# Six layer norms and a head norm: inverse roots moved from GpSimd's power to ScalarE's logarithm and exponential, with a new order of the units

## The chip, the cores and the metric

The kernel runs on one core of one Trainium2 chip. The core has five engines that matter here, each with its own queue of instructions that it serves in order: TensorE (PE in the profile, with its weight loads as PEld), VectorE (DVE), ScalarE (ACT), GpSimd (POOL) and SyncE (SP), which issues the transfers. They wait for each other by semaphores. The metric is the device time of one execution in microseconds (us), the median of several runs.

## The reference

32 graphs of 512 nodes with 256 features go through four layers, each followed by a residual and a layer norm without gain:

```python
def _layernorm(x, axis=-1, eps=1e-5):
    m = jnp.mean(x, axis=axis, keepdims=True)
    v = jnp.var(x, axis=axis, keepdims=True)
    return (x - m) / jnp.sqrt(v + eps)

x = _layernorm(x + _L0_gnn_ref(x, adj, ...))   # 4 heads, attention over edges; norm per head, eps 1e-6
x = _layernorm(x + _L1_gnn_ref(x, adj, W, a))  # 1 head, ELU
x = _layernorm(x + _L2_gnn_ref(x, adj, ...))   # 8 heads, symmetric mask, feed forward of 1024, two norms inside
x = _layernorm(x + _L3_gnn_ref(x, adj, W, a))  # 1 head, leaky
```

So a graph has six norms over 256 features (after layer 0; after layer 1; two inside layer 2; after layer 2; after layer 3) and one norm over the 64 features of each of 4 heads in layer 0. The two in the feed forward that follow each other (the second norm inside layer 2, then that after the residual) have only a gain and an addition between them.

## The kernel before, in words

The kernel first runs `fast_path`, which is right for adjacencies of zeros and ones and for sums that stay in range. It gathers a verdict on the way (`sums`, `ok`), and only where that fails `general_path` runs. In the runs shown only the fast path is executed.

The 512 rows of a graph stand as four blocks of 128 partitions (`R` = 4), features in the free dimension. Every stage of a graph is a Python generator that yields between *units*, small pieces of TensorE work with what belongs to them:

- **edges, x**: load the transposed adjacency in two halves (`adjt`, turned to bytes on ACT with a sum of its entries and of their squares), the features and their transpose.
- **layer 0**: `h0p` (four projections), then for each of four heads `gp` (a row of exponentials spread over the partitions), `pt` (line 393, the unnormalised attention on DVE, four per head), `o` (four times 128x65). Then the head norm (`head_layernorm`) and the norm of the layer (`layernorm`).
- **layer 1** and **layer 3**: `xt1p`/`xt3p` (two units that transpose the normed rows through PE), `h1p`/`h3p` (four projections, copied out of PSUM by ACT on line 333), `gp`, `pt`, `o` (four units, one per block of rows). In layer 1 ACT evaluates a relu and an exponential per block (lines 476, 477), in layer 3 DVE adds the residual (line 674). Then a norm each.
- **mask**: the symmetric mask `a2`, on DVE.
- **qkv**: `xt2p`, `qkp` (four units), `vp`. **attention**: for each of four pairs of heads four units `s` (the scores, exponentials on ACT in line 553, product with the mask on DVE in line 556; the last of the four has the mask `shut` added on PE) and one unit `cp`. **projection**: `ctp` (transposes, also for `ct`, which the prediction calls ctp2 where the two are told apart), `wop`.
- **feed forward**: a norm, `ytp` (transposes), then eight times `f1p` (first product, relu on ACT in line 638 to `ft`) and `f2p` (second product). Then a norm, line 654 (gain), line 655 (residual), and another norm.

A `layernorm` on four blocks: DVE takes statistics of each block (lines 266, 267), adds eps (line 269), GpSimd takes the power -0.5 of a 128x4 tile (line 270), DVE multiplies by the negated mean (line 271), and ACT writes the four blocks one after the other (line 275). `head_layernorm` has sums on DVE, squares on ACT (line 294), a sum of those on DVE (line 295), then scale and eps (line 296), the power of a 128x16 tile on GpSimd (line 297) and a product on DVE (line 298).

**What sets the order.** Some 3.5 graphs are in work at once. Each unit has a place in the table `PLACES`, a number of the planner's time; a unit of graph b stands at `PERIOD * b` plus its place, and the units of all 32 graphs are merged by these numbers:

```python
with tc.manual_schedule(engines={mybir.EngineType.PE}):
    for _ in heapq.merge(*(graph(b) for b in range(B))):
        pass
```

TensorE's instructions stand in exactly that order. Those of the other engines are placed by the tile framework's scheduler, except for a few that are pinned behind the last product (`in_place`). Transfers are all issued by SP.

PSUM has eight banks, given out by stage: two to layers 0 and 1 (with edges and x), four to the middle (qkv, attention, projection), two to feed forward and layer 3 (`bank` takes `n = 4 if stage[0] == "b" else 2`). A product that needs a bank waits until what was in it has been copied out. So within layer 3 the third `h3p` needs the bank of the first, and `gp` that of the third.

Of the kernel before, what the change touches and what calls it, by code (L numbers as in the profile page):

```python
# [27 lines left out]
PLACES = {  # L28
    "edges": [-1440, -1440, -410, 1420],
    "x": [3260],  # L30
    "mask": [16220, 16520, 16600, 17520],
    "layer 0": [
        2410, 3594, 4534, 4534, 5073, 5753, 5753, 5823, 6123, 6123, 6233, 6233, 6603, 6773, 6903,
        7687, 7687, 7777, 8077, 8077, 8157, 8287, 8439, 8439,
    ],
    "layer 1": [11037, 11066, 11277, 11729, 11849, 11879, 12043, 13286, 13554, 14195, 14884],
    "qkv": [17180, 17740, 18270, 18270, 18270, 18990, 19484, 19654, 21635, 21635],
    "attention": [
        20262, 20932, 21922, 21982, 22092, 22092, 22092, 22350, 22350, 23077, 23537, 23537,
        24028, 24208, 24328, 24532, 25064, 25220, 25368, 25943,  # L40
    ],
    "projection": [26801, 26801, 26861, 26911, 27661, 27721, 28721, 29140, 29256, 29848],
    "feed forward": [
        31013, 31120, 32042, 32263, 32263, 32465, 32710, 33771, 33983, 34076, 34284, 34691,
        35070, 35329, 35615, 36103, 36646, 37299,
    ],
    "layer 3": [39714, 39714, 40906, 41226, 41406, 41526, 41526, 42359, 42359, 42379, 42379],
}
# [4 lines left out]
RD_MIN = 1e-25  # L53
RD_MAX = 1e25


# [16 lines left out]
def fast_path(ctx: ExitStack, tc: tile.TileContext, a: dict, out: bass.AP, bad: bass.AP):  # L73
# [21 lines left out]
    VC = DH + 1  # L95
    ND = R * (H + 2 + H2)

    const = ctx.enter_context(tc.tile_pool(name="const", bufs=1))
    latest = [None]
# [25 lines left out]
    nc.vector.tensor_copy(identb, ident)  # L125
    mhalf = const.tile([P, R * H], F32, name="mhalf")
    nc.gpsimd.memset(mhalf, -0.5)
    ok = const.tile([P, ND], F32, name="ok")
    nc.gpsimd.memset(ok, 1.0)
# [129 lines left out]

    def layernorm(y, eps):  # L260

        st = buf([P, R, 6], "bn", "bn", 2)
        mv = buf([P, R, 2], "mv", "mv", 2)
        rs = buf([P, 3, R], "rs", "rs", 2)
        for r in range(R):
            nc.vector.bn_stats(st[:, r, :], y[:, r, :])  # L266
            nc.vector.bn_aggr(mv[:, r, :], st[:, r, :])
        var = mv[:, :, 1]
        nc.vector.scalar_tensor_tensor(rs[:, 0, :], var, eps, var, op0=ALU.add, op1=ALU.max)  # L269
        nc.gpsimd.tensor_tensor(rs[:, 1, :], rs[:, 0, :], mhalf[:, :R], op=ALU.pow)  # L270
        nc.vector.scalar_tensor_tensor(  # L271
            rs[:, 2, :], mv[:, :, 0], -1.0, rs[:, 1, :], op0=ALU.mult, op1=ALU.mult
        )
        for r in range(R):
            nc.scalar.activation(  # L275
                y[:, r, :],
                y[:, r, :],
                AF.Identity,
                bias=rs[:, 2, r : r + 1],
                scale=rs[:, 1, r : r + 1],  # L280
            )

    def head_layernorm(y, eps):

        G = R * H
        yg = y.rearrange("p r (g d) -> p (r g) d", g=H)
        st = buf([P, 3, G], "lnh", "st", 2)
        nc.vector.tensor_reduce(st[:, 0, :], yg, axis=X, op=ALU.add)
        nc.vector.tensor_scalar_mul(st[:, 0, :], st[:, 0, :], 1.0 / HO)
        nc.vector.tensor_sub(yg, yg, st[:, 0, :].unsqueeze(2).to_broadcast([P, G, HO]))  # L290
        for i in range(2):
            g = slice(i * G // 2, (i + 1) * G // 2)
            sq = part("sq").rearrange("p (g d) -> p g d", d=HO)
            nc.scalar.activation(sq, yg[:, g, :], AF.Square)
            nc.vector.tensor_reduce(st[:, 1, g], sq, axis=X, op=ALU.add)
        nc.vector.tensor_scalar(st[:, 1, :], st[:, 1, :], 1.0 / HO, eps, op0=ALU.mult, op1=ALU.add)
        nc.gpsimd.tensor_tensor(st[:, 2, :], st[:, 1, :], mhalf[:, :G], op=ALU.pow)  # L297
        nc.vector.tensor_mul(yg, yg, st[:, 2, :].unsqueeze(2).to_broadcast([P, G, HO]))

# [96 lines left out]

    def layer0(x, xt, at, rd):
        h = yield from project(xt, w0, D + 2 * H, "h0")
# [39 lines left out]
        nc.vector.tensor_add(y, y, h[:, :, :D])  # L438
        head_layernorm(y, 1e-6)
        nc.vector.tensor_mul(y, y, all_rows(gam0))  # L440
        nc.vector.tensor_add(y, y, x)
        layernorm(y, 1e-5)
        return y
# [15 lines left out]

    def layer1(x, at, rd):  # L460
        xt = yield from transposed([x[:, r, :] for r in range(R)], "xt1")
        h = yield from project(xt, w1g, D + 2, "h1")
        ex = buf([P, 2, R, 1], "ex", "ex1", 2)
        nc.scalar.activation(ex[:, 0], h[:, :, D : D + 1], AF.Exp, scale=-1.0)
        nc.scalar.activation(ex[:, 1], h[:, :, D + 1 :], AF.Exp)
        nc.gpsimd.memset(h[:, :, D : D + 1], 1.0)
        gb = yield from along(ex[:, 0], "gb1")
        pt = [kept("pt1", gb, at[:, j, :], ex[:, 1, j, :]) for j in range(R)]

        for r in range(0, R, 2):  # L470
            y, m = (part(n).rearrange("p (r d) -> p r d", d=D) for n in ("relu", "exp"))
            for i in range(2):
                p = yield from attend(pt, h, r + i, "o1")
                rdr = rd[:, r + i : r + i + 1]
                nc.vector.reciprocal(rdr, p[:, D : D + 1])
                nc.scalar.activation(y[:, i, :], p[:, :D], AF.Relu, scale=rdr)
                nc.scalar.activation(m[:, i, :], p[:, :D], AF.Exp, scale=rdr)
            nc.vector.scalar_tensor_tensor(y, m, 1.0, y, op0=ALU.min, op1=ALU.add)
            xr = x[:, r : r + 2, :]
            nc.vector.scalar_tensor_tensor(xr, y, -1.0, xr, op0=ALU.add, op1=ALU.add)  # L480
        layernorm(x, 1e-5)
        return x
# [131 lines left out]

    def feed_forward(x, y):
        layernorm(y, 1e-5)
        yt = yield from transposed([y[:, r, :] for r in range(R)], "yt")
# [4 lines left out]
        for r in range(0, R, 2):  # L622
# [29 lines left out]
            nc.vector.tensor_add(yr, acc, yr)  # L652
        layernorm(y, 1e-5)
        nc.vector.tensor_mul(y, y, all_rows(ln2g))
        nc.vector.tensor_add(y, y, x)
        layernorm(y, 1e-5)
        return y


    def layer3(x, at, rd):  # L660
        xt = yield from transposed([x[:, r, :] for r in range(R)], "xt3")
# [9 lines left out]
        for r in range(R):  # L671
# [4 lines left out]
            )  # L676
        layernorm(x, 1e-5)
        return x
# [11 lines left out]

    def layer0_all(b, x, xt, at, rd):
        if b == 0:
            bcast(bet0, "bet0")
            bcast(gam0, "gam0")
        return (yield from layer0(x, xt, at, rd))

    def layer1_all(b, x, at, rd):
        if b == 0:
            weights13(w1g, "w1g", "a1")
        return (yield from layer1(x, at, rd))  # L700

# [10 lines left out]

    def feed_forward_all(b, x, y):
        if b == 0:
            weights_ff()
        return (yield from feed_forward(x, y))

    def layer3_all(b, x, at, rd):
        if b == 0:
            weights13(w3g, "w3gt", "a3")  # L720
        return (yield from layer3(x, at, rd))

    def graph(b):
        yield PERIOD * b + PLACES["edges"][0]
        rd = sb.tile([P, ND], F32, tag="rd", name="rd", bufs=3)
        rds = [rd[:, ends[i] : ends[i + 1]] for i in range(4)]
        if b == 0:
            xt, x = yield from paced(b, "x", load_x(b))
        at = yield from paced(b, "edges", mask(b))
        if b:  # L730
            xt, x = yield from paced(b, "x", load_x(b))
        x = yield from paced(b, "layer 0", layer0_all(b, x, xt, at, rds[0]))
        x = yield from paced(b, "layer 1", layer1_all(b, x, at, rds[1]))
        a2 = yield from paced(b, "mask", symmetric(b, at))
        qk = yield from paced(b, "qkv", qkv_all(b, x))
        cs = yield from paced(b, "attention", attention(qk, *a2))
        y = yield from paced(b, "projection", attended_all(b, x, cs, rds[2]))
        x = yield from paced(b, "feed forward", feed_forward_all(b, x, y))
        x = yield from paced(b, "layer 3", layer3_all(b, x, at, rds[3]))
        nc.sync.dma_start(out[b].rearrange("(r p) d -> p r d", p=P), x)  # L740
        nc.vector.scalar_tensor_tensor(ok, rd, RD_MIN, ok, op0=ALU.is_ge, op1=ALU.mult)
        nc.vector.scalar_tensor_tensor(ok, rd, RD_MAX, ok, op0=ALU.is_le, op1=ALU.mult)

# [657 lines left out]
```

## Time and profile before

| what | value |
|---|---|
| median of 3 runs | 3909.93 us (3907.24, 3909.93, 3911.33) |
| span of the profiled execution | 3904.6 us (its own time is not listed apart; the three runs lie 2.6 to 6.7 us above the span) |
| PE busy | 3753.3 us, 96% |
| DVE busy | 2674.8 us, 69% |
| ACT busy | 1926.2 us, 49% |
| POOL busy | 346.9 us, 9% |
| mean granted clock of TensorE | 0.983 |
| transfers | 261.20 MB, 23.1% of the DMA engines' time in the one hardware queue |

In the profile each engine's busy time is the union of its instructions. A group is named by its line, engine, operation and `out<-in` by the program's tile names. Lines of PE are all line 102, the helper that issues products, so one goes by the tile names. Behind the bar of a group stand its busy time, the mean of one in ns, and the engine's idle time ahead of it with what ended it. In a timeline the columns are start and length in us, engine, line, operation and tiles; in square brackets the engine's idle time ahead and what released it. A float32 product shows as two passes.

### The profile page before, as it was taken

The page shows a single profiled execution, that of the slowest core. Times are in us where ns is not written, and L with a number is a line of the kernel's source. Part 1 is how long each engine was busy: PE and PEld are TensorE (multiplying, and loading weights), DVE is VectorE, ACT ScalarE, POOL GpSimd, SP SyncE. Part 2 cuts the span into 40 slices and gives each one's busy share as a digit, 9 for nine tenths or more (in the row PEclk, how much of TensorE's full clock was granted, in tenths as well). Part 3 has the DMA queues.
Part 4 walks back from the last instruction along what each step waited for, and adds up shares of the span by engine and source line. Part 5 has one row for each costly group of instructions (what it writes and reads, how often), then busy time and mean ns, then how long its engine had stood idle before and what let it go on. Part 6 is the DMA issues. An engine that isn't in the chain of part 4 may idle for free.

```text
span 3904.6 us, 53602 instructions
## 1 busy us (share of the span) xinstructions
PE 3753.3 (96%) x19238; PEld 2824.5 (72%) x19238; DVE 2674.8 (69%) x5594; ACT 1926.2 (49%) x4257; POOL 346.9 (9%) x266
## 2 busy tenths in 40 slices
PE   5899999999999999999999999999999999999996
PEld 4577777777777777777777777777777777777764
DVE  4667676677677677677677677677777677777653
ACT  2444455444455544455544455545555544555442
POOL 0000010000010001010001010001010001010000
PEclk6899999999999999999999999999999999999998
DMA  3222222222222222222222222222222222221120
GB/s 106 77 73 65 72 58 67 71 76 67 70 60 65 71 76 69 68 62 63 71 76 71 66 63 64 69 76 71 66 65 65 65 76 74 63 67 58 49 54 12
DMA packets 180431, 261.20 MB, mean 67 GB/s; under 512 B 36800, under 2 KB 72768, under 8 KB 180160
## 3 DMA queue, kind: packets, MB, share of 16 engines
q1 hardware_dynamic: 180160, 257.71, 23.1%
q8 instruction: 155, 2.54, 0.3%
q14 instruction: 116, 0.95, 0.1%
HBM read 106.57 MB, written 16.78 MB: 32 GB/s over the span
## 4 chain that ended last, share of the span: by engine, by line
PE 60%; DVE 14%; issue 8%; ACT 5%; POOL 5%; POOLq 0%; ACTq 0%
PE o L102 16%; PE f1p L102 7%; PE f2p L102 6%; PE qkp L102 5%; PE cp L102 5%; DVE pr L556 4%; ACT y L275 4%; POOL rs L270 3%; PE h3p L102 3%; PE s L102 3%; PE h1p L102 3%; PE wop L102 3%; POOL st L297 2%; PE gp L102 2%; PE vp L102 2%
## 5 line engine op out<-in xcount | busy, mean ns | idle before, releaser
L556 DVE TENSOR_TENSOR pr<-pr,a 128x1024 f32<-128x1024 f32 x384 | 459.1, 1216 | 319.3 <-ACT pr L553 319.2
L275 ACT ACTIVATE y<-y,rs 128x256 f32<-128x256 f32 x768 | 398.4, 589 | 438.2 <-DVE rs L271 438.2
L393 DVE SCALAR_TENSOR_TENSOR pt<-gb,ex,at 128x512 f32<-128x512 f32 x768 | 530.6, 744 | 77.6 <-ACT gb L345 77.6
L553 ACT ACTIVATE pr<-s 128x512 f32<-128x512 f32 x1024 | 545.2, 613 | 7.4 <-PE s L102 7.3
L102 PEld LDWEIGHTS o<-hv,pt 128*128 128x128 f32 x4096 | 508.4, 199 | 23.7 <-issue 8.4
L102 PE MATMUL o<-hv,pt 128*128 128x65 f32 x4096 | 502.7, 280 | 9.7 <-DVE pt L393 9.7
L102 PE MATMUL f2p<-wf,ft 128*128 128x256 f32 x2048 | 491.6, 383 | 12.3 <-ACT ft L638 12.2
L102 PE MATMUL cp<-pr,v 128*64 128x512 f32 x2048 | 474.9, 600 | 17.8 <-DVE pr L556 17.1
L102 PE MATMUL f1p<-yt,wf 128*128 128x256 f32 x2048 | 488.9, 381 | 0.3 <-DVE yt L302 0.3
L102 PE MATMUL o<-h,pt 128*128 128x257 f32 x2048 | 482.8, 383 | 3.7 <-DVE pt L393 3.7
L102 PEld LDWEIGHTS o<-h,pt 128*128 128x128 f32 x2048 | 381.5, 190 | 96.0 <-issue 40.6
L270 POOL TENSOR_TENSOR rs<-rs,mhalf 128x4 f32<-128x4 f32 x192 | 246.2, 1282 | 2118.8 <-DVE rs L269 1826.0
L638 ACT ACTIVATE ft<-f1p,cols 128x256 f32<-128x256 f32 x512 | 215.2, 474 | 442.2 <-PE f1p L102 442.2
L102 PEld LDWEIGHTS f2p<-wf,ft 128*128 128x128 f32 x2048 | 380.1, 191 | 69.5 <-ACT ft L638 17.1
L102 PEld LDWEIGHTS f1p<-yt,wf 128*128 128x128 f32 x2048 | 385.3, 191 | 54.5 <-DVE yt L302 0.8
L102 PE MATMUL s<-qk 128*128 128x512 f32 x1024 | 395.1, 481 | 1.6 <-ACT pr L553 1.6
L102 PEld LDWEIGHTS cp<-pr,v 128*64 128x64 f32 x2048 | 133.0, 136 | 286.0 <-issue 194.2
L266 DVE BATCH_NORM_STATS2 bn<-y 128x6 f32<-128x256 f32 x768 | 294.6, 411 | 4.5
L102 PEld LDWEIGHTS s<-qk 128*128 128x128 f32 x1024 | 187.8, 190 | 99.3 <-issue 40.6
L102 PE MATMUL qkp<-xt,wqkv 128*128 128x512 f32 x512 | 231.3, 594 | 0.0
L345 ACT COPY gb<-gp 128x512 f32<-128x512 f32 x192 | 111.5, 581 | 219.4 <-PE gp L102 219.4
L428 DVE RECIPROCAL rd<-o 128x4 f32<-128x4 f32 x128 | 23.4, 183 | 272.7 <-PE o L102 272.7
(134 smaller groups left out, 4582.5 us busy)
## 6 DMA issues: line engine op xcount, KB each, us to landing
qk<-hi SPq DMA_DIRECT2D x1024, 64.0 KB, 2.0
qk<-lo SPq DMA_DIRECT2D x1024, 64.0 KB, 2.0
adjt<-in_adjt SPq DMA_DIRECT2D x64, 512.0 KB, 3.5
adj<-in_adj SPq DMA_DIRECT2D x64, 512.0 KB, 3.6
xt<-in_xt SPq DMA_DIRECT2D x32, 512.0 KB, 3.4
x<-in_x SPq DMA_DIRECT2D x32, 512.0 KB, 4.7
out<-y SPq DMA_DIRECT2D x32, 512.0 KB, 3.0
wf<-in_w1t SPq DMA_DIRECT2D x1, 1024.0 KB, 7.6
```

The lines of the kernel that those rows point to most:

```text
L102: latest[0] = what(*args, **kwargs).ins.name
L266: nc.vector.bn_stats(st[:, r, :], y[:, r, :])
L270: nc.gpsimd.tensor_tensor(rs[:, 1, :], rs[:, 0, :], mhalf[:, :R], op=ALU.pow)
L275: nc.scalar.activation(y[:, r, :], y[:, r, :], AF.Identity, bias=rs[:, 2, r : r + 1], scale=rs[:, 1, r : r + 1],)
L297: nc.gpsimd.tensor_tensor(st[:, 2, :], st[:, 1, :], mhalf[:, :G], op=ALU.pow)
L345: nc.scalar.copy(g, p)
L393: nc.vector.scalar_tensor_tensor(t, g, f, edges, op0=ALU.max, op1=ALU.mult)
L428: nc.vector.reciprocal(rdh, o[:, :, HO:])
L553: nc.scalar.activation(t[:, i, :], s, AF.Exp, scale=QSCALE)
L556: nc.vector.tensor_mul(t, t, edges)
L638: nc.scalar.activation(ft[:, f, :], p[:, f, :], AF.Relu, bias=bf1[:, ff + f : ff + f + 1])
```

## The change

All inverse roots go to ScalarE, as exp(-0.5 ln(variance + eps)). The table set that holds both functions is loaded at the start. The add of eps moves into the logarithm's bias, the head norm's factor 1/64 into the scale of its square. Means and variances of all norms of a graph are kept in one tile `mvs` (three buffers), and at the end of a graph DVE checks that the variances are at most 1e18, beside the check of the denominators that was there. `PLACES` has new numbers for nearly all units, so TensorE's order changes. The scratch for GpSimd's own transfers is set to 8192.

The core of the diff (left out: arguments `mv`, `var` handed through the stages, and the rest of the table):

```diff
 PLACES = {
-    "edges": [-1440, -1440, -410, 1420],
-    "x": [3260],
+    "edges": [-2144, -1150, -1132, 1169],
+    "x": [2625],
...
-    "projection": [26801, 26801, 26861, 26911, 27661, 27721, 28721, 29140, 29256, 29848],
+    "projection": [26272, 26272, 26332, 26382, 27451, 27561, 28792, 29200, 29412, 29811],
     "feed forward": [
-        31013, 31120, 32042, 32263, 32263, 32465, 32710, 33771, 33983, 34076, 34284, 34691,
-        35070, 35329, 35615, 36103, 36646, 37299,
+        30548, 31062, 31829, 32245, 32245, 32541, 32692, 33753, 33965, 34306, 34732, 34800,
+        35052, 35117, 35751, 36541, 37158, 37317,
     ],
-    "layer 3": [39714, 39714, 40906, 41226, 41406, 41526, 41526, 42359, 42359, 42379, 42379],
+    "layer 3": [39718, 39718, 40714, 40734, 40817, 41334, 41569, 42319, 42319, 42339, 42339],
 }
...
+    NL = 6
+    NV = R * (NL + H)
+
+    nc.scalar.preload_act_table_set("natural_log_exp_and_others")
...
-    mhalf = const.tile([P, R * H], F32, name="mhalf")
-    nc.gpsimd.memset(mhalf, -0.5)
-    ok = const.tile([P, ND], F32, name="ok")
+    eps = {}
+    for e in (1e-5, 1e-6):
+        eps[e] = const.tile([P, 1], F32, name=f"eps{e}")
+        nc.gpsimd.memset(eps[e], e)
+    ok = const.tile([P, ND + NV], F32, name="ok")
...
-    def layernorm(y, eps):
+    def inverse_root(out, variance, e):
+        nc.scalar.activation(out, variance, AF.Ln, bias=eps[e])
+        nc.scalar.activation(out, out, AF.Exp, scale=-0.5)
+
+    def layernorm(y, e, mv):
 
         st = buf([P, R, 6], "bn", "bn", 2)
-        mv = buf([P, R, 2], "mv", "mv", 2)
-        rs = buf([P, 3, R], "rs", "rs", 2)
+        rs = buf([P, 2, R], "rs", "rs", 2)
         for r in range(R):
             nc.vector.bn_stats(st[:, r, :], y[:, r, :])
             nc.vector.bn_aggr(mv[:, r, :], st[:, r, :])
-        var = mv[:, :, 1]
-        nc.vector.scalar_tensor_tensor(rs[:, 0, :], var, eps, var, op0=ALU.add, op1=ALU.max)
-        nc.gpsimd.tensor_tensor(rs[:, 1, :], rs[:, 0, :], mhalf[:, :R], op=ALU.pow)
+        inverse_root(rs[:, 0, :], mv[:, :, 1], e)
         nc.vector.scalar_tensor_tensor(
-            rs[:, 2, :], mv[:, :, 0], -1.0, rs[:, 1, :], op0=ALU.mult, op1=ALU.mult
+            rs[:, 1, :], mv[:, :, 0], -1.0, rs[:, 0, :], op0=ALU.mult, op1=ALU.mult
         )
...
-            nc.scalar.activation(sq, yg[:, g, :], AF.Square)
-            nc.vector.tensor_reduce(st[:, 1, g], sq, axis=X, op=ALU.add)
-        nc.vector.tensor_scalar(st[:, 1, :], st[:, 1, :], 1.0 / HO, eps, op0=ALU.mult, op1=ALU.add)
-        nc.gpsimd.tensor_tensor(st[:, 2, :], st[:, 1, :], mhalf[:, :G], op=ALU.pow)
-        nc.vector.tensor_mul(yg, yg, st[:, 2, :].unsqueeze(2).to_broadcast([P, G, HO]))
+            nc.scalar.activation(sq, yg[:, g, :], AF.Square, scale=HO**-0.5)
+            nc.vector.tensor_reduce(var[:, g], sq, axis=X, op=ALU.add)
+        inverse_root(st[:, 1, :], var, e)
+        nc.vector.tensor_mul(yg, yg, st[:, 1, :].unsqueeze(2).to_broadcast([P, G, HO]))
...
         nc.sync.dma_start(out[b].rearrange("(r p) d -> p r d", p=P), x)
-        nc.vector.scalar_tensor_tensor(ok, rd, RD_MIN, ok, op0=ALU.is_ge, op1=ALU.mult)
-        nc.vector.scalar_tensor_tensor(ok, rd, RD_MAX, ok, op0=ALU.is_le, op1=ALU.mult)
+        okd, oks, okv = ok[:, :ND], ok[:, ND : ND + NL * R], ok[:, ND + NL * R :]
+        nc.vector.scalar_tensor_tensor(okd, rd, RD_MIN, okd, op0=ALU.is_ge, op1=ALU.mult)
+        nc.vector.scalar_tensor_tensor(okd, rd, RD_MAX, okd, op0=ALU.is_le, op1=ALU.mult)
+        variances = mvs[:, 1 : 2 * NL * R : 2]
+        nc.vector.scalar_tensor_tensor(oks, variances, VAR_MAX, oks, op0=ALU.is_le, op1=ALU.mult)
+        nc.vector.scalar_tensor_tensor(okv, var, VAR_MAX, okv, op0=ALU.is_le, op1=ALU.mult)
...
-    nc = bacc.Bacc("TRN2", target_bir_lowering=False, num_devices=1)
+    nc = bacc.Bacc("TRN2", target_bir_lowering=False, num_devices=1, dynamic_dma_scratch_size=8192)
```

Around the two norms of the feed forward, TensorE's units in the middle of the run stand as follows, from the built programs (the number is the graph's; `x` with a number means so many in a row):

```
before: 15:f2p 17:o1 16:s+shut 17:o1 16:cp 17:o1 16:ctpx4 17:o1 18:h0p 15:xt3px2 16:ctp2 18:h0p 16:ctp2 18:h0px2 16:wop 15:h3p 16:wop 15:h3p 18:gp0 16:wop 15:h3px2 15:gp3 17:xt2px2 16:wop 18:o0x4
after:  15:f2p 16:s+shut 17:o1 16:cp 17:o1 16:ctpx4 18:h0p 17:o1 18:h0p 16:ctp2x2 15:xt3px2 18:h0px2 15:h3px2 18:gp0 15:h3p 16:wopx2 15:h3p 16:wop 15:gp3 17:xt2p 18:o0x2 16:wop 18:o0 17:xt2p 18:o0
```

## The prediction

> **What bounds the kernel now.** I read the page's busy lines first, then the table by stretches, then PE's waits, then the timeline of one period.
>
> ```profile
> PE 3753.3 (96%) x19238; PEld 2824.5 (72%) x19238; DVE 2674.8 (69%) x5594; ACT 1926.2 (49%) x4257; POOL 346.9 (9%) x266
> ```
>
> ```profile
> 0.00:122.00 122.00, 77.25 (x302) 62.19 (x302) 56.55 (x107) 30.48 (x66) 8.70 (x14) 0.69 0.32 100
> 122.00:244.00 122.00, 112.69 (x572) 81.78 (x572) 78.46 (x143) 49.51 (x105) 8.10 (x5) 0.92 0.28 77
> 244.00:3660.00 3416.00, 3362.45 (x17510) 2539.54 (x17509) 2425.99 (x5078) 1753.29 (x3884) 315.12 (x233) 1.00 0.24 68
> 2044.80:2161.60 116.80, 115.10 (x603) 86.99 (x604) 83.12 (x175) 60.03 (x134) 10.76 (x8) 1.00 0.24 68
> 3782.00:3904.60 122.60, 83.15 (x336) 60.78 (x334) 47.68 (x128) 33.35 (x75) 7.87 (x7) 0.87 0.03 10
> ```
>
> (Stretch, length, then busy us of PE, PEld, DVE, ACT, POOL, granted clock, DMA share, GB/s.) PE is the bound: from 244 to 3660 us it idles 1.6%, at full clock, and the timeline repeats every 116.8 us, one graph. Only the first two and the last stretch are different: 54 us without PE work in them at the start, 39 at the end, and a granted clock of 0.69, 0.92 and 0.87. So the sum has three terms: what PE waits for in a period (about 29 times), the fill and the drain.
>
> The built order of the changed kernel has the same 11,539 matmuls on PE as before, so PE's work itself neither shrinks nor grows; only waits can move. Those of one period, in the timeline:
>
> ```profile
> 1948.93 0.16 DVE L269 SCALAR_TENSOR_TENSOR rs<-mv 128x4 f32<-128x4 f32 x1
> 1949.23 1.01 POOL L270 TENSOR_TENSOR rs<-rs,mhalf 128x4 f32<-128x4 f32 x1 [8.01 <-DVE rd L587]
> ...
> 1950.27 0.16 DVE L271 SCALAR_TENSOR_TENSOR rs<-mv,rs 128x4 f32<-128x4 f32 x1 [0.99 <-POOL rs L270]
> ...
> 1950.47 2.08 ACT L275 ACTIVATE y<-y,rs 128x256 f32<-128x256 f32 x4 [1.11 <-DVE rs L271]
> ...
> 1951.12 0.33 PE L102 MATMUL xt3p<-ident,y 128*128 128x128 f32 x1
> ...
> 1951.61 0.33 PE L102 MATMUL xt3p<-ident,y 128*128 128x128 f32 x1 [0.16 <-ACT y L275]
> ```
>
> ```profile
> 1961.16 0.61 ACT L333 COPY h<-h3p 128x258 f32<-128x258 f32 x2
> ...
> 1961.56 1.61 PEld L102 LDWEIGHTS h3p<-w3g,xt 128*128 128x128 f32 x8 [0.28 <-ACT h L333]
> ...
> 1964.27 0.65 PE L102 MATMUL gp<-ident,ex 128*128 128x128 f32 x4 [0.70 <-ACT ex L665]
> ```
>
> ```profile
> 2027.07 1.99 POOL L270 TENSOR_TENSOR rs<-rs,mhalf 128x4 f32<-128x4 f32 x1 [8.84 <-DVE rs L269]
> 2029.09 0.16 DVE L271 SCALAR_TENSOR_TENSOR rs<-mv,rs 128x4 f32<-128x4 f32 x1 [0.90 <-POOL rs L270]
> 2029.17 1.22 DVE L556 TENSOR_TENSOR pr<-pr,a 128x1024 f32<-128x1024 f32 x1
> ...
> 2030.44 1.94 PE L102 MATMUL cp<-pr,v 128*64 128x512 f32 x8 [0.49 <-DVE pr L556]
> ```
>
> First fence: in the second norm of the feed forward, 1.54 us pass from the start of DVE's add (1948.93) to ACT's first row (1950.47), and 1.01 of them are POOL's power. The transposes xt3p then start 0.49 us apart, as ACT writes row after row, where 0.11 is their pace without a wait: three times 0.38, with 0.17 ahead of the first, is 1.3 us. Second fence: gp (released by line 665's exponentials) starts 2.7 us after the eight h3p passes do, which take 0.22 each: 0.9 of waiting. Third: DVE's line 271 stands ahead of the product that cp needs, and itself waits for a power of 1.99 us; cp's second half starts 2.4 us after its first (2028.02), where 1.8 would do: 0.6. Together **2.8 us a period**.
>
> **The change, part by part.** Rows that price it, from the groups by form (busy us, then mean ns of one):
>
> ```profile
> L270 POOL TENSOR_TENSOR rs<-rs,mhalf 128x4 f32<-128x4 f32 x192 | 246.2, 1282 | 2118.8 <-DVE rs L269 1826.0 <-DVE rd L587 240.0 <-DVE fine L754 21.8
> ...
> L297 POOL TENSOR_TENSOR st<-st,mhalf 128x16 f32<-128x16 f32 x32 | 94.6, 2958 | 1006.5 <-DVE st L296 1006.5
> ...
> L464 ACT ACTIVATE ex<-h 128x4 f32<-128x4 f32 x32 | 6.7, 210 | 0.0
> ```
>
> *Removed:* 224 powers, 340.8 us of POOL, off PE's path except where a norm is awaited; on DVE 192 adds (158 ns) and 32 (168), 35.7 us. *Added:* 448 small activations. The exponential of 128x4 stands in the trace (210, or 192 to 230 for its neighbours); the logarithm does not. Bounds for it: 192 ns, the shortest small ACT row, and 474, the 256-element row with a bias column; I take 210, the row of the same shape. ACT gains 448 x 0.21 = 94 us, from 49% to 52%. On DVE 64 checks of about 0.2 us (row of line 741), 13 us, stand between evacuations of o and cost PE nothing while these are early; without that cover 0.4 a period. The eps columns and the table load fall into the first 12 us, where ACT waits for the first adjacency; no queue of GpSimd carries a DMA in the queue list, so its smaller scratch costs nothing.
>
> *One norm.* Before: aggregate's end to first row 0.03 + 0.16 + 1.0 + 0.16 and hops, 1.57 us (1939.87 to 1941.45, the first norm of the same feed forward). After: logarithm 0.21, exponential 0.21, DVE's product 0.16, four hops of 0.03: 0.7. **0.9 us less**; between 0.6 (logarithm 474) and 1.9 (where the power took 1.99). The head norm saves its 2.9 us power and an add: 65.3 to 68.6 becomes about 0.55, so 2.7.
>
> The Trainium skill (ScalarE: Activation LUTs, What ACT_TABLE_LOAD costs) gives 280 ns plus 0.83 per element for an activation with a pointer bias and 186 for immediates; by it the pair is an estimated 0.47, and a norm saves 0.85 in place of 0.9.
>
> *Where the new waits stand.* The logarithm waits for DVE's aggregate in ACT's queue; behind it stand the exponential, then often a relu of layer 1, a copy of h0p, and the four rows of 2.08 us. ACT serves in order, so whoever is behind waits too. I laid the changed order out by PE's pace per unit (f1p, f2p, o 1.73; cp 3.58; qkp 1.72; h, wop, vp 0.87; one transposition of 512 columns 0.44; s 0.56, last s 1.06), and put DVE's and ACT's rows beside it:
>
> - From the end of f2p to xt3p PE has 14.3 us of work, as before. DVE's add is behind a product (about +1.3), the first norm's rows run +4.6 to +6.7, lines 654 and 655 to +9.4, statistics to +11.5, the second norm's rows from +12.7 to +14.8. The fourth transpose wants its row at +14.6: 0.2 late in place of 1.3.
> - In exchange h3p now follows xt3p after 1.8 us of other work, not 4.4. ACT's relu, exponential, two copies and DVE's copy of the second half come in between: h0p 0.2 and h3p 0.4 late. gp of the next graph needs exponentials that now stand among a logarithm and its exponential: 0.3. The third h3p needs a PSUM bank whose copy stands around four rows (the second fence shows that already: copies from 1961.16, the weight load of h3p held 0.28 for one): 0.2. gp3 has 0.9 us of wop ahead of it, which covers its old 0.9. Together **1.3**.
> - DVE is full for 17 us around gp3 (two sets of four pt at 2.74, 1.22 three times, mask work); o of layer 0 and qkp could find their operand up to 0.45 and 0.4 late. I take 0.3 for both, since a PE that is 1.3 late gives DVE that time.
> - cp: all products of its group stand ahead of the norm's product (line 271's successor) on DVE, and two f products on PE: its 0.6 goes. wop to ytp has 14.8 us in place of 20.0; the rows end about 5 us early.
>
> A period: 2.8 - 1.3 - 0.3 = 1.2 to 1.3 less; 29 x 1.3 = **38 us**. Ends: all 2.8 gone, 81; new waits of 3.3, plus 15.
>
> *Fill:* order and work up to 78 us are the same; PE's 19.7 us gap (58.7 to 78.3) holds head norm and norm: 2.7 + 0.9. The next norm (102.4 to 104.8, power 1.92) leads xt2p, which waited 2.2: 1 less, with 0.9 less PE work ahead. **4.6 us** (3 to 7). *Drain:* two pairs of norms before xt3p (waits 3.3 and 12), the one that kept f2p 3.2 behind ACT's rows, and the last: 1.8 + 1.8 + 1.0 + 0.9, **5.5 us** (2 to 8).
>
> Sum: 38 + 4.6 + 5.5 = 48 off the profiled execution's span, 3904.6 to 3856.5. Its own time isn't listed; the three runs lie 2.6 to 6.7 above the span, the median (3909.9) 5.3. With that, **3862 us**.
>
> **Rivals.** *All waits go and none comes* (period 114.0): 81 + 10, 3819 us. For it: 1.7 idle us are all that the table by stretches shows. Against: h3p's shorter distance.
> *The new waits eat the gain* (period still 116.8): only fill and drain, 3900.
> *Slower: the rows on ACT.* In the built order layer 1's norm of the graph behind stands on ACT between the copies of the first and second h3p. From the point where its product on DVE comes more than 1.3 us after the first copy, its four rows (2.08 us) reach into PE's time and hold the next gp and then the later h3p, whose banks wait for copies: 2 x 2.08, 4.2 in place of 2.8, 29 x 1.4 = 40 more, less 10: 3940. The second fence shows the mechanism at 0.28 us; the full price needs both banks late.
> *It does not stay in one table set.* If each logarithm and the exponential after it loaded tables (1283 ns, once in the trace), 14 a graph, a norm would be 2.6 - 0.9 = 1.7 longer, a pair 3.4: 29 x 3.4 = 99 more, 4009. The built order lists one load in all, so I give it 2%. The Trainium skill (ScalarE: Activation LUTs, Table sets) names a set that holds both functions, and that is the one preloaded.
>
> **Chances.** Forecast 60%, all gone 17%, eaten 10%, rows on ACT 11%, tables 2%. The range 3822 to 3910 leaves out the last two and the lower part of the second, about 0.18. About 0.2% (8 us) is what a measurement of this kernel tells from no change. Faster by more: the first two, less what the first may miss by, and half of the third: 0.80; within: 0.08; slower: 0.12.
>
> **What would show it.** Period: about 115.5 us between like instructions; xt3p at 0.11 us steps; no cp wait on pr; 0.7 us from aggregate to first row; new waits at h3p and gp on ACT's copies; first gap 16 us. Wrong: a logarithm of over 0.4 us, xt3p still in 0.49 us steps, more than one table load, or PE idle in the middle above 1.7 us a period.

## The result and the profile after

| | before | after |
|---|---|---|
| median | 3909.56 us (3907.24 to 3911.33, 4 runs) | 3785.45 us (3782.69 to 3788.34, 4 runs) |
| span of the profiled execution | 3904.6 | 3782.1 |
| period (mean of 16 graphs, first qkp to first qkp) | 116.77 | 113.10 |

The ratio is 0.9682, with a 95% interval of 0.9668 to 0.9696: 124 us less, where the forecast took 48 and the range ended at 3822. The busy line of the page of the changed kernel, and its table by stretches with the columns of the one shown of before:

```profile
PE 3695.1 (98%) x19238; PEld 2832.8 (75%) x19238; DVE 2659.2 (70%) x5434; ACT 2034.2 (54%) x4705; POOL 6.2 (0%) x43
```

```profile
0.00:122.00 122.00, 80.00 (x309) 63.52 (x310) 56.75 (x105) 31.90 (x72) 2.92 (x12) 0.71 0.32 101
122.00:244.00 122.00, 113.58 (x547) 82.00 (x547) 77.90 (x140) 50.56 (x112) 0.10 (x1) 0.87 0.27 73
244.00:3538.00 3294.00, 3291.72 (x17467) 2540.19 (x17466) 2399.53 (x4913) 1842.88 (x4272) 3.04 (x29) 1.00 0.25 70
2044.80:2161.60 116.80, 116.80 (x624) 90.35 (x622) 86.25 (x175) 64.56 (x150) 0.10 (x1) 1.00 0.26 71
3660.00:3782.10 122.10, 89.87 (x375) 63.96 (x373) 49.99 (x126) 41.39 (x98) 0.00 (x0) 0.87 0.03 10
```

In the long middle stretch PE idles 2.3 us of 3294, where it idled 53.6 of 3416. The waits of PE in that stretch (engine, tile, who released it: us in all, times, longest) say the same:

```profile
PE s L106 <- ACT pr L559: 1.4, 1, 1.4
PE f2p L106 <- ACT ft L644: 0.6, 1, 0.6
PE xt3p L106 <- ACT y L282: 0.2, 1, 0.2
```

Each occurs once: no wait is left that comes back with every graph. The places where the prediction saw the three old waits, in the timeline of the changed kernel. First, the second norm of the feed forward:

```profile
1894.92 0.30 ACT L267 ACTIVATE rs<-mvs,eps1e-05_70 128x4 f32<-128x4 f32 x1 [0.87 <-DVE mvs L276]
1895.25 0.21 ACT L268 ACTIVATE rs<-rs 128x4 f32<-128x4 f32 x1
...
1895.55 0.15 DVE L278 SCALAR_TENSOR_TENSOR rs<-mvs,rs 128x4 f32<-128x4 f32 x1
...
1895.74 2.08 ACT L282 ACTIVATE y<-y,rs 128x256 f32<-128x256 f32 x4
...
1898.71 1.04 PE L106 MATMUL xt3p<-ident,y 128*128 128x128 f32 x8
```

The rows end at 1897.82; the fourth transposition starts at 1898.71 + 0.33 = 1899.04 and has its row 1.2 us early. All eight follow at 0.11 us. Second, a period later, the stretch of h3p and gp, with layer 1's four rows between the copies of the first and the second h3p:

```profile
2015.73 0.35 ACT L339 COPY h<-h3p 128x258 f32<-128x258 f32 x1
...
2016.40 2.08 ACT L282 ACTIVATE y<-y,rs 128x256 f32<-128x256 f32 x4 [0.32 <-DVE rs L278]
...
2016.64 1.04 PE L106 MATMUL h3p<-w3g,xt 128*128 128x258 f32 x4
...
2018.39 0.35 ACT L339 COPY h<-h3p 128x258 f32<-128x258 f32 x1
...
2019.24 1.04 PE L106 MATMUL h3p<-w3g,xt 128*128 128x258 f32 x4
```

The rows stand where the slower rival put them, but two units of wop (1.7 us) run over them on PE, and the fourth h3p finds its bank free. Third, cp runs its 16 passes in 3.58 us every time; the half that came 0.6 late before is gone.

Where a period's 3.68 us came from, by the intervals between the starts of PE's passes, summed for each tile and averaged over 16 periods: xt3p 2.08 to 0.87, and 0.17 more ahead of its first pass, which the intervals count with h0p; h3p (with the wait ahead of gp) 4.46 to 3.50; cp 15.05 to 14.34. That is 1.37, 0.97 and 0.72, together 3.06. A small wait at ctp: 0.15. The rest, about 0.5, is mostly no wait but what it costs PE to go from one kind of product to the next (f2p less by 0.80, f1p and s more by 0.52). Such a step takes the same in both kernels (f2p to s 0.03 us, f2p to f1p 0.22, f1p to cp 0.31, from start to start); in the new order f2p is followed by s five times a period, in the old one once.

The sum over the span: the fill (to the third graph's qkp) 4.8 less, 29 periods 107.4 less, the drain 10.3 less; 122.5.

### The profile page after: what moved, and what is told of

It reads as the page before. It is cut to its first block, busy times and chain, and to the rows that moved or that the text cites. A ratio compares the mean times of both kernels' runs of the same rounds, so it can differ in the third digit from the quotient of the medians.

```text
span 3782.1 us, 53679 instructions
## 1 busy us (share of the span) xinstructions
PE 3695.1 (98%) x19238; PEld 2832.8 (75%) x19238; DVE 2659.2 (70%) x5434; ACT 2034.2 (54%) x4705; POOL 6.2 (0%) x43
## 4 chain that ended last, share of the span: by engine, by line
PE 95%; DVE 3%; ACT 1%; issue 0%; DMA 0%; SPq 0%; ACTq 0%; DVEq 0%
PE o L106 24%; PE cp L106 12%; PE f2p L106 12%; PE f1p L106 12%; PE s L106 8%; PE qkp L106 6%; PE h1p L106 3%; PE h3p L106 3%; PE vp L106 3%; PE h0p L106 3%; PE wop L106 3%; PE gp L106 2%; PE ctp L106 2%; PE xt1p L106 1%; PE xt3p L106 1%; PE ytp L106 1%
## 5 line engine op out<-in xcount | busy, mean ns | idle before, releaser
L559 ACT ACTIVATE pr<-s 128x512 f32<-128x512 f32 x1024 | 557.2, 604 | 171.6 <-PE s L106 171.5
L106 PE MATMUL o<-hv,pt 128*128 128x65 f32 x4096 | 510.7, 279 | 10.4 <-DVE pt L399 10.4
L106 PE MATMUL s<-qk 128*128 128x512 f32 x1024 | 412.0, 493 | 4.8 <-ACT pr L559 4.8
L578 ACT COPY cs<-cp 128x512 f32<-128x512 f32 x128 | 75.0, 586 | 188.0 <-PE cp L106 187.8
```

What stands on the lines that cost most here:

```text
L106: latest[0] = what(*args, **kwargs).ins.name
L559: nc.scalar.activation(t[:, i, :], s, AF.Exp, scale=QSCALE)
L578: nc.scalar.copy(t, cp)
```

## The experiments

| kernel | median us | ratio to before (95%) | period us |
|---|---|---|---|
| after | 3785.5 | 0.968 (0.967 to 0.970) | 113.10 |
| e1: new norm, old order | 3912.0 | 1.001 (1.000 to 1.002) | 117.54 |
| e2: old norm, new order | 4021.8 | 1.029 (1.027 to 1.031) | 120.76 |
| e3: after, two more activations in a norm | 3803.3 | 0.973 (0.971 to 0.975) | 113.67 |
| e4: after, six more | 3984.5 | 1.019 (1.018 to 1.021) | 119.41 |
| e5: after, power at the feed forward's end | 3853.6 | 0.986 (0.984 to 0.987) | 115.40 |
| e6: after, power at layer 1 | 3804.4 | 0.973 (0.972 to 0.975) | 113.78 |
| e7: old order, logarithm only at the feed forward's end | 3913.6 | 1.001 (1.000 to 1.002) | 117.12 |
| e8: after, no inverse root | 3980.1 | 1.019 (1.017 to 1.020) | 120.22 |
| e9: after, w1g prepared ahead of layer 0 | 3788.1 | 0.969 (0.968 to 0.971) | 113.10 |
| e10: e5, reciprocal first | 3831.7 | 0.980 (0.979 to 0.982) | 114.67 |
| e11: e8, reciprocal first | 3912.5 | 1.001 (1.000 to 1.002) | 117.86 |
| e12: after, w1g between two heads | 3784.8 | 0.967 (0.966 to 0.969) | 113.09 |
| e13: e1, two places mended | 3876.0 | 0.991 (0.990 to 0.993) | 116.27 |
| e14: e1, three places mended | 3849.8 | 0.985 (0.983 to 0.986) | 115.47 |

The theory at the start (A) was that the shorter norm ends the waits at xt3p and cp and the order the one at gp, and that the new waits did not come because the layout in the prediction was about 1.2 us late. Rivals: the norm alone (B), the order alone (C).

**The two halves of the change, one at a time.** e1 keeps all of the change but the table, in which every list is as before:

```diff
 PLACES = {
-    "edges": [-2144, -1150, -1132, 1169],
+    "edges": [-1440, -1440, -410, 1420],
...
```

> The changed kernel with the table of places of the kernel before, so that the new inverse roots run in the old order of units. Theory A (the shorter norm takes the waits at xt3p and cp away, the new order takes the wait at gp and h3p away): xt3p at about 0.11 us steps, no wait at cp, gp still 0.9 us behind h3p; a period of 114.3 to 115.2 us against 116.8 before and 113.1 after, a time of 3835 to 3855 us. Rival B (the shorter norm alone does it): period 113.1 to 113.5, 3785 to 3800 us. Rival C (the order alone does it): period 116 or more, 3890 us or more.

e2 is the kernel before with the new table.

> The kernel before, with GpSimd's powers, in the new order of units. Each norm is about 0.9 us longer than in the changed kernel, so in the feed forward the last row of the second norm comes about 1.8 us later where the changed kernel's trace leaves 1.2. Theory A: xt3p waits again, the gp3 wait stays away, h3p and gp get new waits; period 114.2 to 116.0 us, 3825 to 3885 us. Rival B (norm alone): period as before, 116.8, about 3905. Rival C (order alone): 113.1 to 113.5, 3785 to 3800.

A and B failed in both runs; e1 came out where C put it, but e2, which C needed at 3785 to 3800, refutes C too. Neither half brings anything. The norm alone gives 3912.0, the order alone loses 112 us, both together gain 124. (The smaller scratch and the check of the variances, which e1 holds too, were not run apart from the norm.) In e1 the wait at cp does go (0.71) and xt3p falls by 0.50, but PE now waits in two new places: 1.1 us at s and f2p, 0.7 at o and h0p; 0.4 more is spent where s goes over to f2p. The first of them in e1's timeline:

```profile
1907.41 2.09 ACT L282 ACTIVATE y<-y,rs 128x256 f32<-128x256 f32 x4
...
1909.38 0.85 ACT L644 ACTIVATE ft<-f1p,cols 128x256 f32<-128x256 f32 x2
...
1909.92 1.99 PE L106 MATMUL f2p<-wf,ft 128*128 128x256 f32 x8 [0.93 <-ACT ft L644]
```

Layer 0's norm is ready sooner, so its four rows now stand in ACT's queue in front of the relu that f2p waits for; with GpSimd's slow power they came after it. In e2 the opposite happens at h3p: the rows of layer 1 come later, stand in front of both copies, and the third h3p waits for its bank:

```profile
2019.12 2.07 ACT L275 ACTIVATE y<-y,rs 128x256 f32<-128x256 f32 x4 [1.35 <-DVE rs L271]
...
2021.33 0.62 ACT L333 COPY h<-h3p 128x258 f32<-128x258 f32 x2
...
2021.73 0.48 PE L102 MATMUL h3p<-w3g,xt 128*128 128x258 f32 x1 [2.15 <-ACT h L333]
```

This is the mechanism of the prediction's slower rival, in another kernel, with one of the two steps of 2.08 us that it was priced at (2.1 to 2.3 here). It is not all that e2 loses: against the changed kernel 2.0 more stand at h0p and the o behind it, 1.2 at xt1p, 0.8 at cp.

**Longer norms in the new order.** e3 and e4 differ from the changed kernel in one loop, of 2 and of 6:

```diff
         nc.scalar.activation(out, out, AF.Exp, scale=-0.5)
+        for _ in range(2):
+            nc.scalar.activation(out, out, AF.Identity)
```

> The changed kernel with two further small activations (128x4, Identity, in place) behind each inverse root, which lengthen each norm by about 0.4 to 0.5 us and give ACT 448 more instructions. Theory A by the margin of 1.2 us that the changed kernel's trace shows at xt3p over two norms: it just holds, under 0.4 us a period, 3785 to 3800 us. Rival D (there was no such margin, and each 0.1 us of norm is paid at the transposes): two times 0.45, 0.9 us a period, 3811 us.

> The changed kernel with six further small activations behind each inverse root, which lengthen each norm by about 1.3 to 1.4 us, more than GpSimd's power cost. Theory A: 2.7 us later at the second norm's last row, less the margin of 1.2, so 1.5 at xt3p, and the new waits that the prediction named at h0p, h3p and gp (0.2 to 1.0) come with it: 1.5 to 2.5 us a period, 3835 to 3865 us. Rival D (no margin): 2.7 and more, 3865 to 3900 us. Rival E (PE has far more room than the layout shows): under 0.5, below 3800 us.

e3 costs 0.57 a period, 0.49 of it at xt3p: between A (under 0.4) and D (0.9). Measured from the h0p ahead, its second norm's rows come 1.5 us later, not 0.9, since relus and exponentials of layer 1 now fall between the small activations; of the 1.5, 0.5 is paid, so about 1.0 of room is confirmed. e4 is far above all three expectations: 6.3 a period, spread over xt3p, xt1p, h0p, h3p and the ctp ahead of xt3p. At xt3p a margin still fits: measured from the same h0p the rows come 4.1 us later, less the 1.0 of room, and 3.2 is paid at xt3p and the ctp ahead of it. The other 3.1, at h3p (1.4), xt1p (1.2) and h0p (0.4), where e3 had shown 0.1 in all, do not follow from it. From here on theory F: an order of units fits one length of norm, because what PE pays is whether rows, copies, exponentials and statistics fall in front of or behind each other on ACT and DVE.

**One norm at a time.** In e5 to e7 some norms take the power again (`pool=True`: add of eps on DVE, power on GpSimd):

```diff
-        layernorm(y, 1e-5, mv[3])
+        layernorm(y, 1e-5, mv[3], True)
...
-        layernorm(y, 1e-5, mv[4])
+        layernorm(y, 1e-5, mv[4], True)
```

> The changed kernel and its order, but the two norms at the end of the feed forward take GpSimd's power again (add of eps on DVE, power of 128x4 on GpSimd); the other norms keep logarithm and exponential. Theory F (an order fits one length of norm: in each place the four rows must fall between ACT's other work, and where they fall in front of a copy or an exponential that PE needs, PE waits up to 2 us): as with all powers in the new order, about 1.9 us a period at h0p, whose bank waits for an exponential of layer 1 that stands behind the first norm's rows, or the same at xt3p: period 114.6 to 115.4, 3835 to 3865 us. Rival G (a norm's length is paid one for one at the transposes that read it): two times 0.9 less the room of 0.4 that the run with half a microsecond more showed, 1.4 a period, at xt3p alone: 114.5, 3829 us.

e6 does it at `mv[1]` alone.

> The changed kernel and its order, but the norm of layer 1 alone takes GpSimd's power. Theory F: its four rows come about 1 us later and then stand in front of the copies of the first two h3p instead of between them; the third h3p waits for a bank: 2.2 to 2.6 us a period, all of it at that place; period 115.3 to 115.8, 3855 to 3875 us. Rival G: the transposes xt2p that read this norm have room of their own, so nothing: period 113.1, 3785 to 3790 us.

e7 has the old table, and `True` everywhere but at `mv[3]` and `mv[4]`.

> The order of the kernel before, with logarithm and exponential at the two norms at the end of the feed forward alone; every other norm and the head norm take GpSimd's power. Theory F: the wait of 1.1 us at f2p that the new norm in the old order brought (layer 0's rows in front of a relu) goes, the wait at cp of 0.7 is back, and xt3p and the o ahead of it stay as in that run, 0.2 worse than before: period 116.6 to 117.2, 3905 to 3925 us. Rival H (the prediction's step: with a shorter norm the wait at xt3p simply goes): 1.2 less a period than before, 115.5, 3870 us.

e8 goes the other way and makes all norms shorter: it leaves out the inverse root and takes a constant in its place, so that nothing is normalised:

```diff
-        inverse_root(rs[:, 0, :], mv[:, :, 1], e)
...
-                scale=rs[:, 0, r : r + 1],
+                scale=fixed[:, r : r + 1],
```

> The changed kernel and its order without any inverse root: logarithm and exponential are left out, and the rows are scaled with the constant 0.5, the head norm too, so what is computed is no norm any more. Each norm is then about 0.55 us shorter, and ACT has 448 instructions less. If PE's own pace is all that is left in the steady stretch, the period stays at 113.0 to 113.1 and only the ends gain (first gap 1.1, drain 1 to 3): 3779 to 3784 us. If waits are still hidden in the groups' lengths, the period falls below 112.9: under 3778. If rows that come earlier stand in front of other work (theory F with the other sign): period above 113.3, 3795 us or more.

e5 came out as F said: 2.30 a period, 1.88 of it at h0p and nothing at xt3p. e7 too: the 1.1 at f2p goes once the other norms, layer 0's among them, have their slow power back. e6 is where F had the right place and the wrong price: 0.69 in place of 2.2 to 2.6, because the rows still fall between two copies, only later, and the bank is 0.43 late:

```profile
1913.83 2.08 ACT L291 ACTIVATE y<-y,rs 128x256 f32<-128x256 f32 x4 [1.54 <-DVE rs L287]
...
1915.81 0.35 ACT L348 COPY h<-h3p 128x258 f32<-128x258 f32 x1
1916.22 1.14 PE L106 MATMUL h3p<-w3g,xt 128*128 128x258 f32 x4 [0.43 <-ACT h L348]
```

e8 decides between a margin and F. Its norms are shorter than the changed kernel's, ACT has less to do, and it is 195 us slower. Its waits: 2.5 a period at h0p and the o behind it, 2.1 at cp, 0.8 at s, 1.0 at h3p. At cp the head norm, ready sooner, puts its gain (line 442) on DVE in front of the product that cp needs:

```profile
1936.36 1.22 DVE L442 TENSOR_TENSOR y<-y,gam_b 128x1024 f32<-128x1024 f32 x1
...
1937.50 1.22 DVE L558 TENSOR_TENSOR pr<-pr,a 128x1024 f32<-128x1024 f32 x1
...
1938.77 1.94 PE L106 MATMUL cp<-pr,v 128*64 128x512 f32 x8 [1.19 <-DVE pr L558]
```

**One instruction's place.** e5 and e8 have the wait at h0p in common. In e5 it reads so:

```profile
1923.71 0.75 DVE L281 BATCH_NORM_STATS2 bn<-y 128x6 f32<-128x256 f32 x2
...
1925.24 0.13 DVE L490 RECIPROCAL rd<-o 128x1 f32<-128x1 f32 x1
...
1925.84 0.47 ACT L492 ACTIVATE exp<-o,rd 128x256 f32<-128x256 f32 x1
...
1926.36 0.92 PE L106 MATMUL o<-h,pt 128*128 128x257 f32 x3 [1.71 <-ACT exp L492]
```

and in the changed kernel:

```profile
1893.02 0.16 DVE L481 RECIPROCAL rd<-o 128x1 f32<-128x1 f32 x1
1893.13 0.75 DVE L275 BATCH_NORM_STATS2 bn<-y 128x6 f32<-128x256 f32 x2
```

A reciprocal of 0.13 to 0.16 us stands behind the second norm's statistics in the one and in front of them in the other; relu, exponential and with them a bank of PSUM hang on it. e10 (on e5) and e11 (on e8) move it by an empty unit ahead of the norm, with PE's order the same. A few small instructions go with it: on DVE a later reciprocal moves up too, in e10 some copies change places, and in e11 the exponential that hangs on the reciprocal stands in front of the norm's four rows on ACT instead of behind them. The edit:

```diff
-        35052, 35117, 35751, 36541, 37158, 37317,
+        35052, 35117, 35751, 36541, 37158, 37317, 38310,
...
         nc.vector.tensor_add(y, y, x)
+        yield
         layernorm(y, 1e-5, mv[4], True)
```

> The run with the power at the two norms at the end of the feed forward, plus an empty unit ahead of the second of them. PE's order is the same; on DVE the second norm's statistics are handed to the scheduler later, so that the reciprocal of the third o of layer 1, which stood behind five of their instructions, now stands ahead of them. Theory F (the 1.9 us at h0p and the o behind it were that one instruction's place: reciprocal late, then relu and exponential, then the bank): the wait falls from 1.9 to under 0.3, the second norm's rows stay where they were, and xt3p now waits for them, 0.8 to 1.6; period 114.2 to 115.0, 3818 to 3845 us. Rival J (the norm's length itself holds PE there, by its rows on ACT): period stays at 115.4, 3850 us or more.

> The run without any inverse root (logarithm and exponential left out, rows scaled with 0.5), plus the same empty unit. In the run without the unit PE waited 2.5 us a period at h0p and the o behind it, 2.1 at cp, 0.8 at s, 1.0 at h3p. Theory F: the 2.5 falls to under 0.3, the rest, which stands elsewhere, stays: period 117.4 to 118.2, 3890 to 3920 us. Rival J: nothing changes, 3975 us or more.

Both times lie where F put them, and J is refuted: at h0p the 1.88 of e5 falls to 0.38 in e10 (just above the 0.3 expected), and the 2.48 of e8 to nothing in e11 (0.48 more at the o behind it); e11 is 68 us faster than e8. In e10 xt3p takes only 0.1, and 0.50 stands at the ctp ahead of it, less than expected.

**The old order, mended.** In e1 three places had stood in the way. e13 takes the rows of layer 0 behind the relu and the reciprocal in front of the statistics; e14 also moves the cast of an adjacency out from between the first norm's exponential and its rows. In e1 they read:

```profile
1942.47 0.22 ACT L268 ACTIVATE rs<-rs 128x4 f32<-128x4 f32 x1
1942.56 1.07 ACT L369 ACTIVATE at<-adjt 128x1024 uint8<-128x1024 int32 x1
...
1943.60 2.07 ACT L282 ACTIVATE y<-y,rs 128x256 f32<-128x256 f32 x4
```

For that, layer 0's norm gets a `yield` ahead of its rows, the second norm of the feed forward one ahead of its statistics as in e10, and the table their places:

```diff
-        7687, 7687, 7777, 8077, 8077, 8157, 8287, 8439, 8439,
+        7687, 7687, 7777, 8077, 8077, 8157, 8287, 8439, 8439, 10640,
...
-        35070, 35329, 35615, 36103, 36646, 37299,
+        35070, 35329, 35615, 36103, 36646, 37299, 38310,
```

e14 has in addition:

```diff
-    "edges": [-1440, -1440, -410, 1420],
+    "edges": [-2144, -1150, -1132, 1169],
```

> The new norm in the old order, with two empty units, so that PE's order is unchanged: one between the inverse root and the rows of layer 0's norm, which takes the rows from in front of the relu that f2p waits for to behind it on ACT; one ahead of the second norm at the end of the feed forward, which takes the reciprocal of the third o of layer 1 from behind that norm's statistics to in front of them on DVE. Without them the period was 117.5 us. Theory F (two instructions' places hide what the shorter norm gains in the old order): the 1.1 at s and f2p and the 0.7 at o and h0p go, 115.6 to 116.2 a period, 3848 to 3870 us, below the kernel before. Rival K (the loss in the old order is spread over the queues and moves elsewhere): 116.8 or more, 3890 us or more.

> The run with the two places mended, plus the third one: the edges units stand at the changed kernel's places, so that the cast of an adjacency (1.07 us on ACT) no longer stands between the exponential of the first norm at the end of the feed forward and its four rows. PE's order is still the old one. With two places mended the period was 116.27 us and xt3p took 2.08 us as in the kernel before. Theory F: the rows come 1.07 us earlier, both norms' sum with them, and xt3p falls to 0.9 to 1.2 us; period 115.1 to 115.5, 3835 to 3855 us; then the old order holds the norm's full gain and the 0.9 at gp is the only wait of size left in it. Rival K (the loss moves on): period 116.0 or more, 3868 us or more.

In e13 both waits are gone to the last 0.1, but 0.5 of them is back at xt3p, whose wait the others had hidden: 116.27, just above what F gave, and 3876, between F and K. e14 takes 0.80 more a period and stands at 3849.8, 59 us under the kernel before, with the old order. Its waits of PE in the middle:

```profile
PE gp L106 <- ACT ex L677: 19.7, 28, 0.7
PE xt3p L106 <- ACT y L287: 4.9, 30, 0.2
```

The first is the old wait at gp, untouched (the prediction's second fence), which the new order removes. xt3p fell to 1.48, not to the 0.9 to 1.2 expected: a 0.60 us exponential of the attention still stands between logarithm and exponential.

**A better version?** The four pieces of layer 1's weights (lines 197 and 200) stand in PE's first gap. e9 hands them out ahead of layer 0, as in the diff, e12 after 14 units of layer 0, between two heads:

```diff
         if b == 0:
             bcast(gam0, "gam0")
+            weights13(w1g, "w1g", "a1")
...
-            weights13(w1g, "w1g", "a1")
```

> The changed kernel, with the preparation of layer 1's weights of the first graph (two products and two sums on DVE, 0.65 to 0.68 us each) handed out ahead of layer 0 instead of behind it. In the changed kernel all four stand between the head norm and the norm in PE's first gap of 16.2 us. If DVE's chain is what sets that gap: 13.5 us, the whole run 2.7 us shorter, 3782 to 3784 us. If another chain does, nothing: 3785 to 3787. Steady stretch the same, 113.1.

> The changed kernel, with the preparation of layer 1's weights handed out between the second and the third head of layer 0 of the first graph, where DVE waits for PE and its operand has landed (at 24.2 us in the run that had it ahead of layer 0, which made the first o wait 5.7 us for that transfer). The first gap falls by 1.9 us, as it did there, to 14.3, and nothing else moves: 3782.5 to 3784.5 us, 0.05% below the changed kernel, less than the runs tell apart; the profile's gap is what decides. If DVE has no room between the heads, the third head's o comes up to 2.6 later and nothing is won.

The gap fell from 16.2 to 14.3 us in both. In e9 it cost more than it brought, since DVE's queue then stood behind a transfer:

```profile
24.18 1.29 DVE L197 TENSOR_TENSOR prod<-w1g,a 128x512 f32<-128x512 f32 x2 [3.47 <-DMA a<-in_a]
...
27.37 2.89 PE L106 MATMUL o<-hv,pt 128*128 128x65 f32 x9 [8.22 <-DVE pt L399]
```

The first o came at 27.37 in place of 21.71, and the span is 3785.3. In e12 the third head's o waits 3.0 us in place of 1.6, and the span is 3782.9 against 3782.1: nothing won. Its runs spread from 3775.3 to 3785.3 us, so their median (3784.8) doesn't set it apart from the changed kernel.

## Why the prediction was wrong

**The step that failed: "Together 1.3" and "I take 0.3 for both", the new waits.** Nothing of them came, 1.6 a period, 46 us over 29 periods. The layout behind them put the second norm's rows at +12.7 to +14.8 us after the last f2p; the trace has them at +11.5 to +13.6. So the transposes were not 0.2 late but 1.0 to 1.2 early, and h0p, h3p, gp and the third bank, all reckoned from there, had that time too. The layout lost it in three steps: the first norm's rows came at +4.1 where it had +4.6, the statistics of the second ended at +10.7 for +11.5, and from there to the first row it took 0.85 where 1.2 was left. And the five small waits were added up as if each came on top of the others, though a PE that waits at one gives the rest that time; e3, whose rows come 1.5 later and so a little after the layout's, pays 0.57 a period, not 1.6. The layout's mechanism was sound: in e2, e4, e5 and e8 waits appear at the places it named (h0p, h3p, gp), at 0.3 to 2.5 us each.

**"2.8 of waits a period"** was a little low for the three that were counted (1.37, 0.97, 0.72: 3.06) and left out 0.6: a small wait at ctp, and the steps between kinds of product. Together 0.9, 25 us over 29 periods. The steps also go against "PE's work itself neither shrinks nor grows; only waits can move": with the same matmuls, the order alone took about 0.5 us a period off PE's own time.

**One norm** was sized well: where nothing else stands in the way, aggregate to first row fell from 1.57 to 0.80 us, 0.77 less where 0.9 was taken, inside the bounds. The logarithm takes more than the 0.21 assumed, as the groups by form of the changed kernel show:

```profile
L267 ACT ACTIVATE rs<-mvs,eps1e-05_70 128x4 f32<-128x4 f32 x192 | 58.4, 304 | 165.6 <-DVE mvs L276 159.6 <-DVE rd L679 5.0
L268 ACT ACTIVATE rs<-rs 128x4 f32<-128x4 f32 x192 | 40.9, 213 | 3.2
```

The pair is 0.52 us; the Trainium skill (ScalarE: Activation LUTs, What ACT_TABLE_LOAD costs) gave an estimated 0.47, nearer than the row that was taken.

**The ends.** First gap 19.66 to 16.19: 3.5 less, 3.6 predicted. Fill 4.8 (4.6). Drain 10.3 where 5.5 was taken: the two last norms' wait at xt3p 1.7 less (1.8 predicted), the pair before it 3.3 (1.8), f2p behind ACT's rows 2.2 (1.0). The remaining 3 us were not taken apart; the last graph's own share of the waits at cp, gp and h3p, which the 29 periods don't hold, is the likely part of them.

**The rivals.** "All waits go and none comes" was the right one, held at 17% for the shorter distance of h3p, and its price was too low by the same 0.9 a period and by 5 us at the drain. The rows on ACT did not come in the changed kernel; in e2 one of their two steps came, at its price. One table load stands in the trace (1.3 us, once), so the tables rival was excluded rightly.

**What no step saw:** the change was costed as a shorter norm plus an order. The experiments show it is a pair: with the old order the norm gains nothing until instructions are moved in two or three places (e1, e13, e14), and with the new order a norm that is longer by a pair of activations or shorter by a pair loses 18 or 195 us (e3, e8). Why the order of ACT and DVE comes out as it does was not tried; the runs show only that moving a reciprocal and what hangs on it (e10, e11), four rows and a reciprocal (e13) or the casts of the adjacency (e14), with PE's order kept, moves the waits.

## What to carry to other kernels

Where several engines serve hand-placed work in order, a step made faster brings its results earlier, and they may then stand in front of something more urgent: a gain of half a microsecond can become a loss of two. So cost such a change from the built order of every engine, asking what stands in front of each reciprocal, copy or relu that frees a bank, and don't add up waits that follow each other, since the first may pay for the next. Where the order of one engine changes, count its steps from one kind of work to another too: they are not waits, and yet they move. Try each half of a paired change alone before calling either of them the cause.

## What the runs showed of the hardware

GpSimd's power took 1.01 us alone, but 1.85 in e6, where it started 0.22 us into an addition of two operands in SBUF on DVE and ended 0.85 after it:

```profile
1911.52 1.22 DVE L415 TENSOR_TENSOR hv<-h,bias_b 128x1024 f32<-128x1024 f32 x1
1911.74 1.85 POOL L274 TENSOR_TENSOR rs<-rs,mhalf 128x4 f32<-128x4 f32 x1 [30.30 <-ACT ex L422]
```

The Trainium skill (SBUF — State Buffer, SBUF: two separate sides) says that such a DVE instruction and one of GpSimd that reads SBUF lock each other out of a shared port for a whole instruction; the two rows agree (blocked to 1912.74, then 0.85). So does the kernel before: of the 128x4 powers, 62 ran into such an instruction of two SBUF operands that had started first, took 1.32 to 1.99 us and ended 0.86 to 0.87 after it; four that ran beside one with an operand in PSUM took 1.01. The logarithms and exponentials of 128x4 that take its place show no such spread: 286 to 329 and 193 to 236 ns over 192 of each.

The granted clock in the second stretch (122 to 244 us) is lower after the change, 0.87 against 0.92, though PE is busier there (113.6 against 112.7 us). That part of the fill may have given some of its gain back; no run tried it apart.
